# Layer 0 of a four-layer graph network: own rows and x are added by accumulating DMAs, nine instead of eight masks stand among the sums, and the steps between the matmuls are set anew

## The chip, the cores and the metric

The kernel runs on one core of one Trainium2 chip. A core has five engines that work side by side, each with its own queue of instructions: TensorE (PE, with its weight loads PEld), VectorE (DVE), ScalarE (ACT), GpSimd (POOL) and SyncE (SP, which here only issues DMAs). Each works its queue off in order; an instruction that waits holds up all that is queued behind it. The metric is the device time of one execution in microseconds (us), the median of several runs. Less is better.

## The reference, cut to what matters

There are N = 2708 nodes with 512 features each (x) and one adjacency matrix of 2708 x 2708 integers (adj). Four layers follow each other, each of the form x = layernorm(x + layer(x, adj)). The change concerns the first:

```python
Ab = A > 0
keep = Ab & (jnp.cumsum(Ab.astype(jnp.int32), axis=1) <= neibor_num)   # the first 64 neighbours of a row
cnt = keep.sum(axis=1, keepdims=True).astype(X.dtype)
nb_mean = (keep.astype(X.dtype) @ X) / jnp.maximum(cnt, 1.0)
xj = jax.nn.leaky_relu(nb_mean @ W_nb.T + b_nb)
xi = jax.nn.leaky_relu(X @ W_line.T + b_line)                          # "own rows"
layer = xi + jnp.where(cnt > 0, xj, 0)
...
x = _layernorm(x + layer, axis=-1)
```

Layer 1 takes the mean over all neighbours (the whole mask, not the first 64), with two weight matrices multiplied by halves of a third, W_comb. Layers 2 and 3 are attention layers, which the change leaves alone.

## The kernel before, in words

The rows are cut into 22 tiles of 128 (the last has 20 rows, `few`). D is 512, KD = 4 is its number of row blocks of 128. y = x @ W_nb.T is made first, so that layer 0's sum is keep @ y. y is held in two parts of a shortened float type, yH and yL, whose sum has the full precision: each matmul of the sums is done twice, once with each (`halves`). A mask tile is 128 rows of adj. It is loaded (`load_mask`, a DMA that POOL issues, 677 KB), counted (`count`, ACT, a sigmoid whose sum goes to cnts), placed (`place`, DVE, a running count that changes all entries behind the 64th neighbour, one scan and one multiplication for each part) and turned, since matmuls need it transposed: on PE (`turn_here`, 22 transposes and signs on ACT) or by a DMA that SP issues (`turn`, followed by `signs` on ACT). The result is maskT, in one byte for each entry.

**Stage A** (loop over the 22 tiles, L423 to L457): for each tile x is turned by PE (xT), multiplied by W_nb.T (kept by `keep_y`: yH by ACT at L272, yL by DVE at L277) and by W_line.T (own rows: DVE adds b_line at L452, POOL issues the store to r0_dram at L453). Beside it HERE = 14 masks are loaded, counted, placed in two halves and turned. The product's results lie in PSUM banks: own rows of an even tile and y of an odd tile, as well as the three banks of `turn_here`, come from four banks `acc` in rotation; the others have a bank each (pm0, pm1). u, the buffer of own rows, exists twice.

**Stage B** (L622 to L651): the sums. The tiles stand in blocks (`cuts`) of 4, 4, 4, 4, 4 and 2. In a block, step j (0 to 21) takes kT, a slice of the mask made by ACT (L471, a relu with the sign changed, so that only the first 64 neighbours remain), and adds its products with yH(j) and yL(j) to the banks of the block's tiles: eight matmuls (L639). At the end of a block ACT copies the banks to u0 to u3, divided by the count (`copy_of`, L620): two at once, two at the next block's first new kT. Between the steps the loop calls generators, one step of each at a time:

- `todo` is `finish` of the block before: fetch own rows (SP), add b_nb (L530), leaky (L229), leaky of own rows, add x to own rows by an accumulating DMA (POOL, L534), then `has` times u plus own rows (L536), the layer norm (`layer_norm`, with a power on POOL at L126), the store of x1 (L538), and the store of x1 as 16-bit words (`store_words`, L149 and L150), which a transposing DMA reads back in stage C.
- `both` is a chain of `other_masks` (the remaining eight masks: load, count in two halves, place in four, turn), `weights1` (the two weights of layer 1: rows of W_nb and W_self turned by PE at L139 and multiplied by halves of W_comb) and `vectors` (small vectors for layers 2 and 3).

PE's own order in stage A is written out by hand (`pe`, each of its instructions behind the one before); elsewhere a scheduler sets each engine's order by priority, and `tc.issue_after(x)` puts what stands in it behind x in the order.

**Stage C** (L652 to L672): layer 1's products, two for each tile (L300), from x1's words (`from_words`; the turned words are joined by ACT at L161). Behind it stage D makes layer 1's sums.

Of the kernel before, what the change touches and what calls it, by code (L numbers as in the profile page):

```python
# [20 lines left out]
P = 128  # L21
# [11 lines left out]
def kernel(  # L33
# [203 lines left out]
    with ExitStack() as phase:  # L237
# [68 lines left out]
        HERE = NT - 8  # L306
        cuts = [(b, min(b + 4, NT)) for b in range(0, NT, 4)]
        turns = range(NT)

        def load_mask(i, m):  # L310
            n = rows(turns[i])
            nc.gpsimd.dma_start(m[:n, :N], adj[turns[i] * P:turns[i] * P + n, :], max_dma_last_dim=N * 2)
            return m
# [43 lines left out]
        with ExitStack() as ph:  # L357
# [64 lines left out]
            due, stored = [], {}  # L422
            for t in range(NT):  # L423
# [18 lines left out]
                if now:  # L442
                    with tc.issue_after(stored[t - 1].ins) if t > 2 else nullcontext():
                        m = masks(counted)
# [3 lines left out]
                    with tc.issue_after(lows[t].ins):  # L448
                        place(counted, m, places, 0, 2)
                pm = product(xT, n, wlT, 1, pe, None if t % 2 else sums())  # L450
                u = sm.tile([P, D], F32, name="u")
                low = nc.vector.tensor_add(u[:n], pm[:n], b_line[:n])  # L452
                stored[t] = nc.gpsimd.dma_start(r0_dram[t * P:t * P + n, :], u[:n])  # L453
# [9 lines left out]
        with ExitStack() as ph:  # L463
# [10 lines left out]
            def other_masks():  # L474

                def room(i):
                    r = (ahead.tile([P, 2 * KD * (D + 2 * H)], BF16, name="w", tag="w", bufs=1) if i % 2 else
# [6 lines left out]
                got, left = {HERE: room(HERE)}, iter(())  # L484
                into = weight2.rearrange("p k c -> p (k c)").bitcast(BF16)[:, :NT * P].rearrange("p (t n) -> p t n", n=P)
                for _ in range(5):
                    yield
                for i in range(HERE, NT):
                    if i + 1 < NT:
                        got[i + 1] = room(i + 1)  # L490
# [8 lines left out]
                    for part in range(4):  # L499
                        place(i, m, places, part, 4)  # L500
# [6 lines left out]
                    for _ in left:  # L507
                        pass
                    turn(i, m, into)
                    left = chain(signs(i, into), map(twins, turns[i:i + 1], [turns[i] + 1]))  # L510
                    yield
                    if i < LAST:
                        yield
# [1150 lines left out]
```

## Time and profile before

| | us |
|---|---|
| median of 3 runs | 2873.31 (2872.43 to 2873.46) |
| the profiled execution | 2874.96 |
| its span, first to last instruction | 2873.2 |
| mean granted clock of PE | 0.996 |
| stage A | 0 to 188.8 |
| stage B | 188.8 to 455 |
| stage C | 455 to 614 |
| DVE busy, 0:50, 50:100, 100:150 | 30.65, 42.64, 43.13 |
| PE busy, 0:50, 50:100, 100:150 | 46.55, 46.45, 49.30 |

The profile is of one execution. Times in its views are microseconds from the span's start, unless marked ns. A line of the timeline holds start, duration, engine, line of the code, operation, output<-input and number; in brackets the engine's idle time ahead of it and what ended that. Durations of matmuls overlap, since they are pipelined: the time from start to start is what counts. A line of the windows holds the window, its length, busy time and number for PE, PEld, DVE, ACT and POOL, PE's granted clock (1.00 is full speed), the busy share of the DMA engines, and GB/s. A line of the waits holds engine, tile and line that waited, what it waited for, and the total, the number of times and the longest.

### The profile page before, as it was taken

The numbers are of one execution on the slowest core, as the hardware profiler recorded it, in microseconds if no ns is written. First come the engines' busy times: TensorE is split into PE (matmuls) and PEld (weight loads), VectorE is DVE, ScalarE is ACT, GpSimd is POOL, SyncE is SP. The second block draws the span as 40 slices with busy tenths as digits, with TensorE's granted clock in tenths as the row PEclk, the third lists the DMA queues.
The fourth block names the chain that finished last, engine by engine and source line by source line (L and its number), as shares of the span: only waits on it lengthen the run. The fifth ranks groups of instructions, "written<-read, shape, count | busy, mean of one in ns | idle before, by whom it ended". The sixth has DMA issues, their size and how long they took to land. (4 is left out here: it accounts for less than half of the span.)

```text
span 2873.2 us, 35718 instructions
## 1 busy us (share of the span) xinstructions
PE 2801.1 (97%) x13910; PEld 1556.9 (54%) x13910; DVE 1992.8 (69%) x2372; ACT 1525.4 (53%) x1754; POOL 294.1 (10%) x457
## 2 busy tenths in 40 slices
PE   9999999999999999999999999999999999999998
PEld 5458764458886434444466433444385555555565
DVE  6856755643336999999978999999954435445342
ACT  4646642232336999999956999999950000000011
POOL 1112421111110000000021000000300010100001
PEclk9999999999999999999999999999999999999999
DMA  7745657533323011111152110111161000000000
GB/s 181 151 105 124 148 145 172 123 96 122 107 82 69 27 38 38 42 48 42 36 175 84 41 41 36 56 36 35 35 173 52 4 26 15 26 15 16 15 19 25
DMA packets 203654, 202.64 MB, mean 71 GB/s; under 512 B 126823, under 2 KB 151724, under 8 KB 203476
## 3 DMA queue, kind: packets, MB, share of 16 engines
q1 hardware_dynamic: 167592, 122.05, 16.2%
q0 software_dynamic: 24880, 74.01, 9.5%
q10 hardware_dynamic: 11004, 4.22, 0.6%
q8 instruction: 111, 1.82, 0.3%
q14 instruction: 67, 0.55, 0.1%
HBM read 137.90 MB, written 55.66 MB: 67 GB/s over the span
## 5 line engine op out<-in xcount | busy, mean ns | idle before, releaser
L894 DVE SCALAR_TENSOR_TENSOR e<-v_bc,ucol,maskT 128x1408 f32<-128x1408 f32 (+3 forms) x798 | 1133.0, 1483 | 315.5 <-PE pn L1295 307.3
L923 ACT ACTIVATE c<-e,bcol 128x1300 fp8e4<-128x1300 f32 (+2 forms) x688 | 956.7, 1412 | 61.7 <-DVE e L894 16.8
L1095 PE MATMUL po<-e,R 128*64 128x512 f32 (+3 forms) x4224 | 893.9, 549 | 25.8 <-DVE e L894 23.6
L1095 PEld LDWEIGHTS po<-e,R 128*64 128x64 f32 (+1 forms) x4224 | 333.7, 136 | 553.0 <-issue 390.0
L1295 PE MATMUL pn<-e,R 128*128 128x512 f32 (+1 forms) x1008 | 396.4, 557 | 0.8
L1295 PEld LDWEIGHTS pn<-e,R 128*128 128x128 f32 x1008 | 177.8, 190 | 195.5 <-issue 181.2
L1224 ACT ACTIVATE w<-pl,b 128x256 f32<-128x256 f32 (+1 forms) x88 | 40.9, 465 | 365.7 <-PE pl L1222 365.7
L126 POOL TENSOR_TENSOR ln_rs<-ln_rs,half 128x1 f32<-128x1 f32 (+1 forms) x88 | 56.7, 644 | 1321.6 <-DVE ln_rs L125 1300.4
L815 PE MATMUL pm<-w,xT 128*128 128x264 f32 (+1 forms) x704 | 164.1, 388 | 3.4 <-ACT xT L141 1.3
L686 PE MATMUL acc<-yH,mf 128*128 128x512 f32 x418 | 162.9, 390 | 0.0
L686 PE MATMUL acc<-yL,mf 128*128 128x512 f32 x418 | 162.8, 390 | 0.0
L1222 PE MATMUL pl<-lin 128*128 128x256 f32 (+1 forms) x704 | 152.9, 372 | 0.6 <-DVE lin L1124 0.6
L1247 PE MATMUL pl<-lin,w 128*128 128x512 f32 x336 | 150.8, 593 | 0.0
L1222 PEld LDWEIGHTS pl<-lin 128*128 128x128 f32 x704 | 129.5, 190 | 31.0 <-issue 15.8
L815 PEld LDWEIGHTS pm<-w,xT 128*128 128x128 f32 (+1 forms) x704 | 129.9, 190 | 28.9 <-ACT xT L141 3.5
L683 ACT CAST mf<-maskT 128x1024 fp32r<-128x1024 fp8e4 (+1 forms) x66 | 64.5, 978 | 142.9 <-PE acc L686 140.1
L995 PE MATMUL pd<-c,parts_c 128*12 128x384 fp8e4 (+2 forms) x2688 | 128.4, 307 | 0.0
L471 ACT ACTIVATE kT<-maskT 128x512 fp32r<-128x512 fp8e4 x121 | 75.9, 629 | 97.5 <-PE acc L639 80.3
L639 PE MATMUL acc<-yH,kT 128*128 128x512 f32 x304 | 123.0, 404 | 3.8 <-ACT kT L471 2.9
L300 PE MATMUL acc<-w,xT 128*128 128x512 f32 (+1 forms) x256 | 117.3, 602 | 5.1 <-ACT xT L161 2.7
L639 PE MATMUL acc<-yL,kT 128*128 128x512 f32 x304 | 119.9, 394 | 0.0
L1313 ACT COPY lin<-pn 128x512 f32<-128x512 f32 (+1 forms) x12 | 5.8, 538 | 204.6 <-PE pn L1295 204.6
(291 smaller groups left out, 3007.9 us busy)
## 6 DMA issues: line engine op xcount, KB each, us to landing
v_bc<-v_dram SPq DMA_DIRECT2D x16, 704.0 KB
x_dram<-u POOLq DMA_DIRECT2D x42, 256.0 KB, 2.4
v_bc<-v_dram SPq DMA_DIRECT2D x16, 650.0 KB
m<-in_adj_dram POOLq DMA_DIRECT2D x14, 677.0 KB, 7.1
rows<-in_x_dram SPq DMA_DIRECT2D x21, 256.0 KB
r_dram<-u POOLq DMA_DIRECT2D x21, 256.0 KB, 3.5
rows<-r_dram SPq DMA_DIRECT2D x21, 256.0 KB
rows<-in_x_dram POOLq DMA_DIRECT2D x21, 256.0 KB, 4.8
```

The costliest lines, as they stand in the source:

```text
L300: order(nc.tensor.matmul(pm[:m], xT[:, k, :m], w[:, k, :], start=(k == 0), stop=(k == KD - 1)))
L471: made = nc.scalar.activation(kT, maskT[:, j:j + g, b[0] * P:b[0] * P + w], AF.Relu, scale=-1.0)
L639: nc.tensor.matmul(pa[t], kT[:, (t - b[0]) * P:(t - b[0] + 1) * P], y(j), start=(j == 0 and y is yH), stop=(j == LAST))
L686: nc.tensor.matmul(pa, mf[:, j - g0, :], y(j), start=(j == 0 and y is yH), stop=(j == LAST))
L815: nc.tensor.matmul(pm[a][:m, :D // 2 + heads], xT[:, k, :m], w[:, k, a, :D // 2 + heads], start=(k == 0), stop=(k == KD - 1))
L894: self.made = nc.vector.scalar_tensor_tensor(e[:, :w], v[:, :w], ucol[:, j, h:h + 1], maskT[:, j, c0:c0 + w], op0=OP.max, op1=OP.mult)
L923: nc.scalar.activation(c[:, :w], e[:, :w], AF.Sigmoid, bias=bcol[:, j, h:h + 1], scale=STEP, saturate=False)
L995: pe(nc.tensor.matmul(p[32 * g:32 * g + 12, :c1 - c0], parts_c[:, j, h, :], c[:, c0:c1], start=(i == 0 and h == hs[0]), stop=(i == NT - 1 ...
L1095: pe(nc.tensor.matmul(po[i][HO * k:HO * k + HO, :c1 - c0], R2[at, j, h * HO:(h + 1) * HO], e[at, a:a + c1 - c0], start=(i_ == 0), stop=(i_ ...
L1222: nc.tensor.matmul(pl[:, :w], self.lin1[:, k, f * P:(f + 1) * P], h[:, k, :w], start=(k == 0), stop=(k == KD - 1))
L1247: nc.tensor.matmul(pl[:n], gT[:, f, (t - t0) * P:(t - t0) * P + n], self.lin2[:, f, :], start=(f == 0), stop=(f == KF - 1))
L1295: nc.tensor.matmul(pn[k][:, :w], R2[at, j, k * P:(k + 1) * P], e[at, :w], start=(j == 0), stop=(j == NT - 1))
```

## The change

It touches layer 0 and the start of layer 1's weights:

- Stage A counts, places and turns 13 masks instead of 14, stage B nine instead of eight. PE turns seven in stage A instead of eight, DMAs six as before. The masks now come at tiles 1 to 3, 5 to 7, 9 and 10, 12 to 14, 16 and 17 (before: 1 to 4, 6 to 8, 10 to 13, 15 to 17).
- The leaky step on own rows is done in stage A, ahead of their store. The store of a tile is issued while the next tile is worked on, behind the next mask's load on POOL's queue.
- `finish` adds b_nb (times `has`), does the leaky step and then adds x and, two steps later, own rows to u in DRAM-to-buffer DMAs that accumulate. Nothing of own rows is fetched; the fetch on SP, L530, L536 and the leaky step on own rows are gone. The layer norm of a tile comes five steps, the store of its words six steps after its first. A step comes at odd j: 11 in a block.
- Of a block's end copies, two are made at once, one at j = 1 and one at j = 2, each behind the step's matmuls.
- The next mask is loaded behind the first of the four places of this one instead of ahead of this one's count. `twins` (a small copy of the mask's last rows) are sent later, in pairs.
- `weights1` begins at the first place of the last mask, and fetches its row blocks of weights one ahead; in SP's order three of them stand ahead of the last two masks' turns. The roles of two buffers (`w` and `spare`) are exchanged.
- `vectors` begins in stage C.

The diff, without what only renames a buffer's turn:

```diff
-        HERE = NT - 8
+        HERE = NT - 9
...
+            def store_own():
+                for t, u in own:
+                    stored[t] = nc.gpsimd.dma_start(r0_dram[t * P:t * P + rows(t), :], u)
+                own.clear()
+
             for t in range(NT):
...
                 if now:
-                    with tc.issue_after(stored[t - 1].ins) if t > 2 else nullcontext():
+                    with tc.issue_after(stored[t - 2].ins) if t > 2 else nullcontext():
                         m = masks(counted)
...
+                with tc.issue_after(loads[-1].ins):
+                    store_own()
                 pm = product(xT, n, wlT, 1, pe, None if t % 2 else sums())
                 u = sm.tile([P, D], F32, name="u")
-                low = nc.vector.tensor_add(u[:n], pm[:n], b_line[:n])
-                stored[t] = nc.gpsimd.dma_start(r0_dram[t * P:t * P + n, :], u[:n])
+                nc.vector.tensor_add(u[:n], pm[:n], b_line[:n])
+                low = leaky(u[:n], u[:n])
+                own.append((t, u[:n]))
+                if t >= LAST - 1:
+                    store_own()
...
             def other_masks():
...
-                for _ in range(5):
+                for _ in range(3):
                     yield
                 for i in range(HERE, NT):
-                    if i + 1 < NT:
-                        got[i + 1] = room(i + 1)
...
                     for part in range(4):
-                        place(i, m, places, part, 4)
+                        placed[:] = [place(i, m, places, part, 4)]
+                        if part == 0 and i == LAST:
+                            next(made_weights)
+                        elif part == 0:
+                            got[i + 1] = room(i + 1)
+                        if part == 0:
+                            for k in pairs:
+                                twins(k, k + 1)
+                            pairs.clear()
...
+                    if i > HERE:
+                        pairs.append(i - 1)
                     turn(i, m, into)
-                    left = chain(signs(i, into), map(twins, turns[i:i + 1], [turns[i] + 1]))
+                    left = signs(i, into)
                     yield
-                    if i < LAST:
-                        yield
+                    if HERE + 1 < i < LAST:
                         yield
...
             def finish(ts_, us):
-                r0s = early(1, len(ts_), lambda i: fetched(r0_dram, ts_[i], rows(ts_[i])))
-                for i, t in enumerate(ts_):
-                    n, u, r0 = rows(t), us[t], r0s(i)
-                    nc.vector.tensor_add(u[:n], u[:n], b_nb[:n])
-                    leaky(u[:n], u[:n])
-                    with tc.issue_after(low.ins):
-                        leaky(r0, r0)
-                    nc.gpsimd.dma_start(r0, x[t * P:t * P + n, :], accum_op=OP.add)
+                adds = []
+
+                def added(i, src):
+                    t = ts_[i]
+                    adds.append(nc.gpsimd.dma_start(us[t][:rows(t)], src[t * P:t * P + rows(t), :], accum_op=OP.add))
+
+                for i in range(len(ts_) + 6):
+                    with tc.issue_after(placed[0].ins) if placed else nullcontext():
+                        if i < len(ts_):
+                            t, n, u = ts_[i], rows(ts_[i]), us[ts_[i]]
+                            nc.vector.scalar_tensor_tensor(u[:n], b_nb[:n], has[:n, t:t + 1], u[:n],
+                                                           op0=OP.mult, op1=OP.add)
+                            leaky(u[:n], u[:n])
+                            added(i, x)
+                        if 0 <= i - 2 < len(ts_):
+                            added(i - 2, r0_dram)
+                        with tc.issue_after(adds[-1].ins):
+                            if 0 <= i - 5 < len(ts_):
+                                t = ts_[i - 5]
+                                n, u = rows(t), us[t]
+                                layer_norm(sm, u[:n], n, u[:n])
+                                nc.gpsimd.dma_start(x1_dram[t * P:t * P + n, :], u[:n])
+                            if 0 <= i - 6 < len(ts_) and ts_[i - 6] < LAST:
+                                t = ts_[i - 6]
+                                even = t % 2 == 0 and t < cuts[-1][0]
+                                store_words(words if even else ahead.tile([P, D], F32, name="rows", bufs=3),
+                                            x1_words, t, us[t])
                     yield
-                    nc.vector.scalar_tensor_tensor(u[:n], u[:n], has[:n, t:t + 1], r0, op0=OP.mult, op1=OP.add)
-                    layer_norm(sm, u[:n], n, u[:n])
-                    nc.gpsimd.dma_start(x1_dram[t * P:t * P + n, :], u[:n])
-                    yield
-                    store_words(r0 if t % 2 or ts_ == range(*cuts[-1]) else words, x1_words, t, u)
-                    yield
...
             def weights1():
...
-                order = [(w, m) for w in (l1_w_nb, l1_w_self) for m in range(KD)]
+                w_rows = early(1, 2 * KD, lambda i: fetched((l1_w_nb, l1_w_self)[i // KD], i % KD, P))
                 load_weight(first, l1_w_comb[D:2 * D, :], nc.sync)
-                nxt_rows = fetched(*order.pop(0), P)
+                w_rows(0)
...
-                        xT = transposed(ahead, ps_tr, nxt_rows, P, "xT")
-                        nxt_rows = fetched(*order.pop(0), P) if order else None
+                        xT = transposed(ahead, ps_tr, w_rows(i * KD + m), P, "xT")
...
+                        elif i and m == 0:
+                            twins(LAST - 1, NT)
...
-            todo, both = iter(()), chain(other_masks(), weights1(), vectors())
+            made_weights = weights1()
+            todo, both = iter(()), chain(other_masks(), made_weights)
...
-                        with tc.issue_after(nxt_made.ins):
-                            while copies:
-                                copy_of(*copies.pop(0))
                     kT = kTs.pop(0)
...
-                    if j % 3:
+                    if copies and j:
+                        with tc.issue_after(nxt_made.ins):
+                            copy_of(*copies.pop(0))
+                    if j % 2:
                         next(todo, None)
...
+            both = vectors()
+            placed.clear()
```

More of the change, by code (lines that the diff above doesn't have):

```diff
@@ L301, in product @@
             return pm
-        HERE = NT - 8
+        HERE = NT - 9
         cuts = [(b, min(b + 4, NT)) for b in range(0, NT, 4)]
         turns = range(NT)
+        loads = []
         def load_mask(i, m):
             n = rows(turns[i])
-            nc.gpsimd.dma_start(m[:n, :N], adj[turns[i] * P:turns[i] * P + n, :], max_dma_last_dim=N * 2)
+            loads.append(nc.gpsimd.dma_start(m[:n, :N], adj[turns[i] * P:turns[i] * P + n, :], max_dma_last_dim=N * 2))
             return m
@@ L421 @@
             counted = turned = 0
-            due, stored = [], {}
+            due, stored, own = [], {}, []
+            def store_own():
+                for t, u in own:
+                    stored[t] = nc.gpsimd.dma_start(r0_dram[t * P:t * P + rows(t), :], u)
+                own.clear()
             for t in range(NT):
@@ L476, in room @@
                 def room(i):
-                    r = (ahead.tile([P, 2 * KD * (D + 2 * H)], BF16, name="w", tag="w", bufs=1) if i % 2 else
+                    r = (ahead.tile([P, 2 * KD * (D + 2 * H)], BF16, name="w", tag="w", bufs=1) if (i - HERE) % 2 else
                          st.tile([P, 2 * KD * D], BF16, name="spare", tag="spare"))
@@ L482, in room @@
                     return m, r[:, NT * P:NT * P + N // 4 + 1]
-                got, left = {HERE: room(HERE)}, iter(())
+                got, left, pairs = {HERE: room(HERE)}, iter(()), []
                 into = weight2.rearrange("p k c -> p (k c)").bitcast(BF16)[:, :NT * P].rearrange("p (t n) -> p t n", n=P)
-                for _ in range(5):
+                for _ in range(3):
                     yield
                 for i in range(HERE, NT):
-                    if i + 1 < NT:
-                        got[i + 1] = room(i + 1)
                     m, places = got.pop(i)
@@ L545 @@
-            made1, signs_left = [], []
+                adds = []
[23 more added lines that the diff above has]
+                                            x1_words, t, us[t])
+                    yield
@@ L546 @@
+            made1, signs_left, placed = [], [], []
             acc, words = (sm.tile([P, D], F32, name="u") for _ in range(2))
@@ L549, in weights1 @@
             def weights1():
-                first, second = st.tile([P, KD, D], F32, name="spare", tag="spare"), weight2
+                first, second = weight(), weight2
                 bcs = []
-                order = [(w, m) for w in (l1_w_nb, l1_w_self) for m in range(KD)]
+                w_rows = early(1, 2 * KD, lambda i: fetched((l1_w_nb, l1_w_self)[i // KD], i % KD, P))
                 load_weight(first, l1_w_comb[D:2 * D, :], nc.sync)
-                nxt_rows = fetched(*order.pop(0), P)
+                w_rows(0)
                 nc.sync.dma_start(bias1, bcast(l1_b_comb, D))
@@ L561, in weights1 @@
                 for i, (bc, wc) in enumerate(zip(bcs, (first, second))):
-                    dst = weight() if i == 0 else st.tile([P, KD, D], F32, name="spare", tag="spare")
+                    dst = weight() if i else st.tile([P, KD, D], F32, name="spare", tag="spare")
                     made1.append(dst)
```

## The prediction

> **What bounds the kernel now.** I read the page from the top. Its first part gives the engines, its second the slices.
>
> ```profile
> span 2873.2 us, 35718 instructions
> PE 2801.1 (97%) x13910; PEld 1556.9 (54%) x13910; DVE 1992.8 (69%) x2372; ACT 1525.4 (53%) x1754; POOL 294.1 (10%) x457
> ```
>
> TensorE (PE) is busy 97% of the span, so only 72 us of PE's idle time and the time at a lower clock can be won without taking work from PE. The chain of work that ended last is of no help here: every share in it is 0%. I went to the windows instead, PE's busy time and granted clock (the PEclk column, behind POOL's) in stretches of 50 us. The change touches what runs from 0 to about 610 us. The stages are A (products, masks) to 189 us, B (layer 0's sums) to 455, C (layer 1's products) to 614.
>
> ```profile
> 50.00:100.00 50.00, 46.45 (x160) 22.83 (x159) 42.64 (x35) 28.66 (x39) 8.24 (x17) 0.97 0.80 155
> 200.00:250.00 50.00, 49.54 (x218) 40.43 (x217) 31.15 (x50) 30.18 (x48) 9.68 (x15) 1.00 0.39 85
> 300.00:350.00 50.00, 46.29 (x195) 37.01 (x194) 33.90 (x60) 29.17 (x46) 19.04 (x23) 0.97 0.71 150
> 350.00:400.00 50.00, 45.66 (x182) 34.06 (x181) 37.47 (x65) 23.99 (x42) 13.26 (x19) 0.97 0.58 150
> 450.00:500.00 50.00, 45.72 (x113) 21.66 (x112) 30.54 (x49) 11.68 (x15) 7.22 (x11) 0.97 0.77 164
> ```
>
> Four windows lose 3.5 to 4.3 us of PE and show the clock at 0.97, the others next to nothing. The waits of PE in the first 700 us, by releaser (total, times, longest), name them:
>
> ```profile
> PE ps_tr L139 <- DMA rows<-in_L_gnn_W_nb_dram: 4.3, 1, 4.3
> PE acc L336 <- DVE u L452: 3.6, 1, 3.6
> PE acc L639 <- ACT kT L471: 2.9, 1, 2.9
> PE acc L300 <- ACT xT L161: 2.7, 1, 2.7
> PE acc L300 <- DVE ln_rs L125: 1.6, 1, 1.6
> ```
>
> Each happens once. A stall costs more than its idle time. PE's timeline shows a sum's matmuls issued every 0.23 us; behind the 2.93 us of idle before 319.22 they come every 0.43 us, eight in a row:
>
> ```profile
> 319.22 0.50 PE L639 MATMUL acc<-yH,kT 128*128 128x512 f32 x1 [2.93 <-ACT kT L471]
> ...
> 320.25 0.63 PE L639 MATMUL acc<-yH,kT 128*128 128x512 f32 x1
> 320.68 0.63 PE L639 MATMUL acc<-yL,kT 128*128 128x512 f32 x1
> ```
>
> So that stall costs 2.93 + 8 x 0.20 = 4.5 us. Behind 3.55 us of idle at 90.45 and behind 2.70 us at 487.15 a product takes 5.40 us for 3.60 to 3.70 (1.7 and 1.8 more); behind 1.58 us at 477.35 it takes 3.67. I count the after-effect only for idle times above 2 us. The Trainium skill, "TensorE: Matmul & The Clock Gate", section "What's actually happening", states that the clock halves after an idle window of about 3.4 us and that the window runs freely. Idle times of 2.70 and 2.93 us have halved it here. Were shorter ones than 3.4 us free of it, the gain below would be 3.4 us smaller; I go by the rows.
>
> **What can go, by stage.** Stage A: 3.55 + 1.7 at 90.45, 0.69 at 120.50 (L340): 5.9. Stage B: 0.46 (236.18), 0.27 (271.94), 0.79 (313.08, ACT's copy L620), 4.5 (319.22), 4.34 + 1.6 for the weight rows at 385.03, 0.69 at 439.73: 12.6. Stage C: 1.58 (477.35), 2.70 + 1.8 (487.15), 0.17 and 0.63 (510.09, 514.38): 6.9. Together 25.4 us. One mask fewer is turned by PE (L336, 22 transposes): rows of 1.42 to 1.49 us, 1.45. **The ceiling of the gain is 26.9 us**; all else that the change moves lies beside PE and counts only where it makes PE wait.
>
> **Stage A.** DVE loses one mask's placing (two scans, two multiplies: 2.98 + 3.03 + 2 x 0.86 = 7.7) and gets 22 leaky steps (L229, 0.68 each, 0.60 from start to start: 13). It was busy 42.6 of 50 us in the two worst windows, so this isn't free. The stall at 90.45 came so: DVE stood 2.87 us before 69.59 for a count (L317), whose mask load stood on POOL's queue behind the store of own rows (the largest POOL wait of this stage is for u of L452, 116 us in 20 times). Then it worked without a gap through two and a half masks to 90.40, when u of the tile (L452) came free, and the third bank of the transposes needed it at 86.89. After the change the load stands before that store, so I take the 2.87 off; the run of masks 12 to 14 has the same form. From the first scan to u of its third tile: 8.4 (first mask with y's subtraction) + 9.55 (second: 7.7 with u's addition, y's subtraction and the new leaky at 0.6 each) + 3.7 (scan, addition) = 21.65 us, where before it was 20.8. So u comes 20.8 - 21.65 + 2.87 = 2.0 us earlier than before, and 3.55 becomes **1.5 us**, below what halves the clock. In the run of tiles 5 to 7 the turn comes at tile 7 behind one and a half masks, 12.1 us: I take 0.7. At the even tiles (4, 10, 18, 20) the third bank is that of two tiles ago, no wait. Kept: 2.2 of 5.9. Bounds: 0 (both waits vanish) to 2 x (3.55 + 1.7) = 10.5 (the count comes no earlier, both stalls are full ones). The store of own rows a tile later waits for nothing that PE needs: u has two buffers, the next use is two tiles (14 us) on, and a store lands 3.5 us after issue.
>
> **Stage B, block starts.** Before, copies 2 and 3 of a block's end (L620) and a count's half could stand together ahead of kT: on ACT one copy waited 1.86 us for an old x_dram store and then a 1.41 us count went before kT:
>
> ```profile
> 316.56 0.69 ACT L620 ACTIVATE u<-pm,rkeep 128x512 f32<-128x512 f32 x1 [1.86 <-DMA x_dram<-u]
> 317.14 1.41 ACT L317 ACTIVATE w<-w,gate 128x1354 bf16<-128x1354 bf16 x1
> 318.46 0.19 ACT L317 ACTIVATION_READ_ACCUMULATOR w<-w,gate 128x1 f32 x1
> 318.55 1.14 ACT L471 ACTIVATE kT<-maskT 128x512 fp32r<-128x512 fp8e4 x2
> ```
>
> After it, step j of a block (eight matmuls, 1.815 us) gets one thing each: copies 0 and 1 and kT(1) at the end (0.6 each: 1.84 us against 1.815), copy 2 with half a count and kT(3) (5.1 against 5.4), copy 3 with the other half (0.64 + 1.6 + 0.6 more: 7.75 against 7.26). That is 0.5 us of wait at four blocks, **2.0 us**, and no store is waited for, since a finish ends at step 19 of 22. Bounds: 0 and 4 x 0.8 + 4.5 (one such stall remains) = 7.7.
>
> **Stage B, finishing.** Per tile DVE loses the addition of b_nb (0.67), a leaky (0.68) and L536's wait for the landing (18.4 us of DVE's idle in 20 times); the addition with has takes L536's place (0.74). SP loses 21 fetches of own rows. POOL gets 22 accumulating DMAs. An issue of this kind takes 0.91 us (321.36), the landing a median of 4.8. Two sums to one tile must follow each other, so POOL's order holds x(0), x(1), the load of the next mask, own rows (0) (waits for x(0)'s landing), (1), x(2), own rows (2), x(3), own rows (3) (waits 4.8 us), and behind these the power of the layer norm (L126) and the stores. PE needs none of them until stage C, except through masks and weights. The mask load, 6.3 to 8.0 us, is issued 14.5 us or more (eight steps) ahead of its count: **6.5 us to spare**. The ninth mask's work (DVE 8.5, ACT 3.2 + 3.1) lies beside PE, DVE being busy 31 to 37 of 50 us here and relieved of 28. Cost 0; with the cover gone see the first rival.
>
> **Stage B, weights.** The rows of W_nb, issued at 382.10 behind the fetches of own rows and awaited at 385.03, now stand (three of four) on SP ahead of the last two masks' turns, and own rows are no longer there: 5.9 and 0.7 go. One place is tight, the fourth row block, which needs the buffer of tile 13's words. These are made at step 15 of the block (15 x 1.815 + two weight products of 3.43 = 34 us), their store lands 3.9 us on, the fetch takes 2.9: 41 us. PE asks at step 17 (17 x 1.815 + 3 x 3.43 + transposes 1.4 = 43). I keep 0.5 us; bounds 0 and 5.9.
>
> **Stage C.** vectors() starts here, so its first loads no longer stand on SP before the transposes of x1_words: ACT stood 13.0 us for one at 485.94. And DVE no longer holds for the accumulating DMA (2.69 us before 473.35) that led to the 1.58. Seven loads now come between two of the transposes, about 28 us before PE needs the later one. I keep 1.0 of 6.9; bounds 0 and 6.9.
>
> **Sum.** Kept: 2.2 + 2.0 + 0.5 + 1.0 = 5.7. Gain 26.9 - 5.7 = 21.2 us. The profiled execution took 2874.96 (span 2873.2, 1.8 around it), so it would be 2853.8; the median of the runs shown is 2873.31, 1.65 lower, and by it **2852.1**, which I give as 2852.0. All lower bounds: 2846.4. All upper bounds (10.5 + 7.7 + 5.9 + 6.9 = 31 kept): 2877.4.
>
> **Rivals.** *One: POOL is late with the mask loads, and the change is slower.* Two more accumulating DMAs a tile, with waits for their landings in the queue, hold POOL; the load of the next mask comes more than 6.5 us late; the count stands at ACT's head and kT behind it. Place: steps 1 and 2 of a block. Price: the row at 319.22, 4.5 us, for each of eight loads, 36 us: 2852 + 36 = 2888. It decides from about five such stalls on. For it: POOL's wait for L126 is 119 us in 22 times, and landings went up to 9.1 us. Against: in POOL's order nothing that waits for a landing stands directly ahead of the load at a block's start, POOL is busy 10%, and its issues take 0.91 us beside a busy DVE. 15%. The Trainium skill speaks against the change here: "SBUF — State Buffer", section "SBUF: two separate sides", says that GpSimd can't write the descriptors of a DMA that it issues while VectorE runs certain operations, and that a DMA issued on SP is immune. By that page, estimated at one scan (1.6 us) for each of 22 DMAs that leave SP, POOL would lose 35 us in all, 6 a block, which is about the time to spare; no row here shows such a block.
>
> *Two: the stalls go halfway.* Stage A's fuller DVE stalls PE in full at tiles 7 and 15 (10.5 for 2.2 us, 8.3 more), or one stall of 4.5 us stays at a block start as well: 2860 to 2865, say 2863. For it: DVE 85% busy in stage A with 5 us net to do on top. Against: its idle time of 13.1 us for counts, which the earlier loads shorten. 17%.
>
> *Three: the stalls only move.* Four long ones made 20 of the 25 us, each by one late buffer; a new order can have four others: 2870. 11%.
>
> **How the numbers follow.** Forecast, 13 to 27 us gained: 57%. Rival two: 17%. Three: 11%. One: 15%. About 0.2% (5.7 us) is what a measurement of this kernel can tell from no change. Faster: 0.57 + 0.17 = 0.74; same 0.11; slower 0.15. The range leaves out the slower case and a little beyond the ceiling: 2845 to 2874, which takes in the third rival and the upper bounds but for the last 3 us.
>
> **What would show it.** Right: the windows 300 to 400 and 450 to 500 at 49 us or more of PE and clock 1.00; no wait of PE for W_nb rows or for xT L161; at most two waits of 1 to 2 us for u in stage A; DVE without the waits for own rows and x. Wrong: PE waits for kT with ACT waiting for a mask load (rival one); a wait above 2 us at the turns of tiles 7 or 15 (two); a new wait of 3 us or more for weights or xT (three).

## The result and the profile after

The changed kernel is slower: 2881.8 us (median of 22 runs, 2876.1 to 2886.92) against 2874.31 (22 runs, 2870.09 to 2878.24); the ratio is 1.0024, 95% interval 1.0018 to 1.0031. Forecast were 2852.0 and a range from 2845 to 2874, so the result lies outside it. The profiled execution took 2884.09 us, 2.3 above the median. The head of its page:

```profile
span 2882.3 us, 35604 instructions
...
PE 2802.1 (97%) x13888; PEld 1557.6 (54%) x13888; DVE 1984.2 (69%) x2355; ACT 1525.6 (53%) x1756; POOL 306.2 (11%) x479
```

DVE and PE have fewer instructions, as the diff says, and PE is as busy as before in spite of 22 fewer transposes: a product at half the clock counts as busy for longer (5.40 us instead of 3.60 to 3.70). The windows (busy time of PE, PEld, DVE, ACT and POOL, then granted clock, DMA share and GB/s):

```profile
50.00:100.00 50.00, 50.00 (x172) 24.59 (x171) 47.45 (x43) 31.94 (x42) 8.27 (x17) 1.00 0.79 166
100.00:150.00 50.00, 46.92 (x161) 23.13 (x160) 42.42 (x39) 26.62 (x35) 7.41 (x15) 0.97 0.83 170
250.00:300.00 50.00, 45.75 (x194) 37.09 (x193) 29.54 (x46) 29.55 (x47) 20.21 (x31) 0.97 0.85 160
350.00:400.00 50.00, 43.02 (x163) 32.41 (x162) 33.11 (x61) 23.20 (x40) 18.33 (x26) 0.90 0.78 147
450.00:500.00 50.00, 45.61 (x121) 23.37 (x120) 27.04 (x45) 13.34 (x17) 8.52 (x13) 0.97 0.83 176
```

The loss at 50 to 100 has moved to 100 to 150, the sums lose in 250 to 300 what they didn't before, and 350 to 400 is worse, with the clock at 0.90. PE's waits in the first 700 us:

```profile
PE acc L672 <- ACT kT L484: 9.6, 3, 4.4
PE pm L672 <- ACT kT L484: 7.3, 3, 3.6
PE acc L338 <- DVE u L462: 3.1, 1, 3.1
...
PE acc L300 <- DVE u L705: 1.2, 1, 1.2
```

The waits for the rows of W_nb, for xT and for ln_rs are gone, as forecast. In their place PE waits six times for kT, 16.9 us, four of them for 3.4 to 4.4 us with half clock behind each (1.7 to 2.2 us more). One place shows PE's wait and what ACT did ahead of it, at the start of the third block:

```profile
281.26 0.50 PE L672 MATMUL acc<-yH,kT 128*128 128x512 f32 x1 [4.25 <-ACT kT L484]
```

```profile
274.12 0.62 ACT L484 ACTIVATE kT<-maskT 128x512 fp32r<-128x512 fp8e4 x1
278.60 0.69 ACT L656 ACTIVATE u<-acc,rkeep 128x512 f32<-128x512 f32 x1 [3.85 <-DMA x_dram<-u]
279.18 1.41 ACT L319 ACTIVATE spare<-spare,gate 128x1354 bf16<-128x1354 bf16 x1
280.50 0.19 ACT L319 ACTIVATION_READ_ACCUMULATOR spare<-spare,gate 128x1 f32 x1
280.59 1.14 ACT L484 ACTIVATE kT<-maskT 128x512 fp32r<-128x512 fp8e4 x2
```

It is the picture of 316 us in the kernel before: a copy waits for the store of x1 out of its buffer, then a count goes ahead of kT. The finish of the block before isn't done. POOL and DVE, in that block, show why:

```profile
241.93 0.85 POOL L552 DMA_DIRECT2D u<-in_x_dram  x1 [1.06 <-DVE u L229]
249.51 0.85 POOL L552 DMA_DIRECT2D u<-r_dram  x1 [6.73 <-DMA u<-in_x_dram]
250.04 1.19 POOL L552 DMA_DIRECT2D u<-in_x_dram  x1
256.91 0.86 POOL L552 DMA_DIRECT2D u<-r_dram  x1 [5.67 <-DMA u<-in_x_dram]
257.47 1.51 POOL L126 TENSOR_TENSOR ln_rs<-ln_rs,half 128x1 f32<-128x1 f32 x2
...
273.37 0.58 POOL L569 DMA_DIRECT2D x_dram<-u  x1 [0.88 <-DVE u L128]
```

```profile
248.92 0.15 DVE L125 TENSOR_SCALAR ln_rs<-ln_mv 128x1 f32<-128x1 f32 x1
258.41 1.15 DVE L128 TENSOR_SCALAR u<-u,ln_mv,ln_rs 128x512 f32<-128x512 f32 x2 [9.34 <-POOL ln_rs L126]
```

The own-row add of the third tile waits 6.7 us at POOL's head for that tile's x to land; the fourth tile's x is queued behind it, its own rows wait 5.7 us more, and behind these stand the powers of the first two tiles, ready since 249. DVE waits 9.3 us at its own head for them, and the next mask's places, the layer norms of the last two tiles and their stores (the last issued at 273.4) come behind that. That store lands at 278.5, and the copy at 278.60 waited for it: the finish ends some 9 us after the next block has begun (its first copies stand at 269.3).

It is so all through stage B. The longest waits of POOL and DVE for landings and powers there (186 to 470 us), of the changed kernel first, then of the kernel before:

```profile
POOL u L552 <- DMA u<-in_x_dram: 62.0, 14, 8.4
```

```profile
DVE u L128 <- POOL ln_rs L126: 35.3, 13, 12.4
DVE ln_st L121 <- DMA u<-r_dram: 20.5, 7, 6.6
```

```profile
DVE u L128 <- POOL ln_rs L126: 9.2, 17, 1.1
```

The stages in the profiled executions (us). Stage A ends with PE's first matmul of the sums, C with its first of layer 1's sums; the end of B is taken 0.7 us behind the last matmul of layer 0's sums, in every row alike:

| | stage A ends | B lasts | C lasts | behind C |
|---|---|---|---|---|
| before | 188.8 | 267.1 | 157.6 | 2259.7 |
| after | 186.5 | 278.7 | 151.9 | 2265.2 |

B lost 11.6, A and C won 2.3 and 5.7. Behind C, where no instruction differs, 5.5 us were lost, and 3.1 of them go with the kernel, not with the execution: from DVE's last instruction, behind which only the last store is left, to the end of the span it is 11.0 to 11.2 us in all four kernels that add x and own rows of every tile by accumulating DMAs (the changed one, e1, e5, e9 below), 9.9 in e13, which does so for half of the tiles, 8.6 and 8.8 in e10 and e7, which store own rows so, and 7.7 to 8.0 in the other eleven. No run shows why. The other 2.4 us arise around 2100 us; e14, whose late layers are those of the kernel before, loses as much there, so I count them as a difference between executions.

### The profile page after: what moved, and what is told of

Read it like the earlier page. It is cut to its first block, busy times and chain, and to the rows that moved or that the text cites. A ratio compares the mean times of both kernels' runs of the same rounds, so it can differ in the third digit from the quotient of the medians.

```text
span 2882.3 us, 35604 instructions
## 1 busy us (share of the span) xinstructions
PE 2802.1 (97%) x13888; PEld 1557.6 (54%) x13888; DVE 1984.2 (69%) x2355; ACT 1525.6 (53%) x1756; POOL 306.2 (11%) x479
```

## The experiments

**Theory A**: two accumulating DMAs in series for each tile hold POOL's queue and DVE, and a finish outlasts its block. **Rival B**: the counts, which now stand at block starts ahead of kT, are the cause whatever the finish does. **Rival C**: the DMA traffic is too dense. Each group of runs had the kernel before beside it, whose median lay between 2874.3 and 2876.0 us; so differences of under 2 us between rows say nothing. Stages are those of the one profiled execution. Medians, ratios to the kernel before (95% intervals) and stages (us):

| run | median us | ratio | A ends | B | C |
|---|---|---|---|---|---|
| e1 layer norm freed | 2876.84 | 1.0002 (0.9993-1.0011) | 185.0 | 271.4 | 153.5 |
| e2 no own rows | 2858.76 | 0.9938 (0.9925-0.9952) | 187.0 | 257.7 | 153.7 |
| e3 own rows fetched | 2862.52 | 0.9953 (0.9939-0.9966) | 187.9 | 265.1 | 150.3 |
| e4 before, vectors later | 2873.86 | 0.9998 (0.9989-1.0007) | 190.0 | 266.2 | 157.0 |
| e5 POOL reordered | 2875.28 | 0.9999 (0.9989-1.0009) | 186.0 | 264.1 | 150.3 |
| e6 = e3, xT copies later | 2864.21 | 0.9961 (0.9947-0.9975) | 186.7 | 254.7 | 159.5 |
| e7 one add, early copy of x | 2874.13 | 0.9995 (0.9986-1.0004) | 199.3 | 255.3 | 153.2 |
| e8 before, stage A's part | 2863.76 | 0.9952 (0.9939-0.9966) | 188.9 | 256.8 | 154.8 |
| e9 copies 2, 3 later | 2901.02 | 1.0089 (1.0073-1.0104) | 186.5 | 294.7 | 154.3 |
| e10 one add, x copied by tile | 2866.67 | 0.9968 (0.9955-0.9980) | 193.9 | 259.9 | 151.4 |
| e11 before, leaky step only | 2867.05 | 0.9966 (0.9953-0.9979) | 188.7 | 257.0 | 154.6 |
| e12 = e3, eight masks | 2878.88 | 1.0011 (1.0003-1.0020) | 189.4 | 266.3 | 163.3 |
| e13 last two tiles fetched | 2870.01 | 0.9986 (0.9978-0.9995) | 185.0 | 267.9 | 151.4 |
| e14 = e8, turn moved | 2863.27 | 0.9958 (0.9945-0.9971) | 188.7 | 256.2 | 155.8 |
| e15 = e3, turn moved | 2859.81 | 0.9948 (0.9935-0.9961) | 183.9 | 263.2 | 150.3 |
| e16 = e15, xT and vectors | 2852.72 | 0.9918 (0.9905-0.9932) | 183.3 | 258.9 | 150.3 |

### The second accumulating DMA: e1, e2, e3, e5, e13

e1 frees the layer norm from the last own-row add:

```diff
-                        with tc.issue_after(adds[-1].ins):
+                        with nullcontext():
```

> The changed kernel, but the layer norm is no longer ordered behind the last own-row add: on POOL the powers of a block's first two tiles now stand ahead of the own-row add of its fourth tile. Theory A (two accumulating DMAs in series for each tile hold POOL, and with it the powers, DVE and the end of a block's finish): DVE's wait for the power, 9.3 us at 258 us, falls to about 4, the store that ACT's copy waits for comes some 5 us earlier, and the time falls by 6 to 12 us from the changed kernel's 2882, to 2870 to 2876. Rival B (the counts that now stand at the start of each block ahead of kT on ACT are the cause, whatever the finish does): within 2 us of 2882. Rival C (the DMA traffic is too dense and landings are long): within 3 us.

5.0 us faster than the changed kernel, just short of what A expected of it, outside what B and C did. DVE's longest wait for a power fell to 4.1 us, as A had it, and PE's waits for kT at the first three block starts to 0.5 us or less; but at 371 us PE waits 7.5 us for kT behind the signs of a late turn (3.6 at 379 in the changed kernel), so the gain is what is left of two changes. e2 leaves the own-row adds out:

```diff
-                        if 0 <= i - 2 < len(ts_):
-                            added(i - 2, r0_dram)
```

> The changed kernel without the own-row adds of layer 0 (own rows are left out of the output; one accumulating DMA a tile is left, x). Theory A: POOL's waits for a landing (66 us in 16 times) go, the copies at block starts wait for no store, stage B loses 15 to 20 us of its 278, time 2862 to 2867. Rival B: 2879 to 2882, the waits for kT stay. Rival C: lower too, by the share of the traffic, about 5 us.

23 us faster. The counts stand where they stood; PE's waits for kT in e2:

```profile
PE acc L670 <- ACT kT L484: 2.9, 3, 1.6
...
PE pm L670 <- ACT kT L484: 0.3, 1, 0.3
```

3.2 us for 16.9: **B falls** (own rows are missing in e2's output). e3 fetches own rows on SP and adds them on DVE ahead of the layer norm (0.67 us a tile):

```diff
+                r0s = early(0, len(ts_), lambda i: fetched(r0_dram, ts_[i], rows(ts_[i])))
...
-                        if 0 <= i - 2 < len(ts_):
-                            added(i - 2, r0_dram)
+                        if 0 <= i - 4 < len(ts_):
+                            r0s(i - 4)
...
+                                nc.vector.tensor_add(u[:n], u[:n], r0s(i - 5))
                                 layer_norm(sm, u[:n], n, u[:n])
```

> The changed kernel, but own rows are fetched by a plain DMA of SP's queue one step ahead and added by DVE ahead of the layer norm (0.67 us a tile); x is still added by the accumulating DMA. The same bytes move as in the changed kernel. Theory A: like the run without own rows but for 22 x 0.67 us of DVE beside PE: 2862 to 2870. Rival B: 2879 to 2884. Rival C: as the changed kernel, 2879 to 2884, since the traffic is the same.

19.3 us faster with the same bytes: **C falls**, as far as the number of bytes goes. In the profiled executions 13.6 of it lie in B, 1.6 in C and 5.4 behind C, while A is 1.4 longer. What differs is in the issues (last number: median us to landing), first of the changed kernel, then of e3:

```profile
u<-in_x_dram POOLq DMA_DIRECT2D x21, 256.0 KB, 6.2
u<-r_dram POOLq DMA_DIRECT2D x21, 256.0 KB, 5.2
```

```profile
rows<-r_dram SPq DMA_DIRECT2D x21, 256.0 KB
u<-in_x_dram POOLq DMA_DIRECT2D x21, 256.0 KB, 4.6
```

One accumulating DMA a tile lands in 4.6 us, and nothing is queued behind its landing; two take 6.2 and 5.2 in series. POOL's waits for x to land, 62.0 us in 14 times within 186 to 470 us, are not there in e3. Is it the place on POOL's queue or the two landings? e5 keeps both adds and puts them in a better order:

```diff
-                adds = []
+                adds, xs_ = [], []
...
                             added(i, x)
+                            xs_.append(adds[-1])
                         if 0 <= i - 2 < len(ts_):
-                            added(i - 2, r0_dram)
-                        with tc.issue_after(adds[-1].ins):
+                            with tc.issue_after(xs_[-1].ins) if i >= len(ts_) else nullcontext():
+                                added(i - 2, r0_dram)
+                        with nullcontext():
```

> The changed kernel with both accumulating DMAs kept, but on POOL the own-row adds of a block's third and fourth tile stand behind the x add of the fourth, and the powers of the first two tiles ahead of the last own-row add. Theory A in the form that the order on POOL's queue is the price: POOL's waits for a landing inside stage B fall from 53 us (the run with the freed layer norm) to about 35, stage B from 271 to 267 us, time 2870 to 2874. Theory A in the form that two landings one after the other are the price, wherever they stand: as the run with the freed layer norm, 2875 to 2879.

2875.28: by the time, the form with the two landings (2875 to 2879). But its profiled execution was the fastest of 11 (2867.1, up to 2883.48), and there POOL's waits for a landing are down to 20.4 us, further than the form with the order had forecast, PE's waits for kT are about those of e3 (0.3, 0.3, 0.3, 1.4 and 5.2 us for 0.2, 0.3, 0.3, 1.2 and 6.9), and B is as short as e3's. That execution loses only behind C (2264.8 us for 2259.8 in e3). Where the slower ten lose more is in no trace. So the price of the second add as a whole is shown, 19 us; a better order on POOL wins 5.0 (e1) to 6.5 us (e5) of it; that the rest is the second landing is argued, not shown. Nor does a run fetch own rows by a plain DMA on POOL's queue, which would tell the queue from the accumulation. e13 fetches own rows for a block's last two tiles only:

```diff
+                r0s = early(0, len(ts_), lambda i: fetched(r0_dram, ts_[i], rows(ts_[i])) if i > 1 else None)
...
-                        if 0 <= i - 2 < len(ts_):
+                        if 0 <= i - 2 < min(2, len(ts_)):
                             added(i - 2, r0_dram)
+                        if 0 <= i - 4 < len(ts_):
+                            r0s(i - 4)
...
+                                if i - 5 > 1:
+                                    nc.vector.tensor_add(u[:n], u[:n], r0s(i - 5))
```

> The changed kernel, where own rows of a block's first two tiles are still added by accumulating DMAs, and those of its other two are fetched by SP and added by DVE. If the late end of a finish (the third and fourth tile's chain of two landings, with the powers of the first two tiles queued behind it) is the price, this is as good as fetching all: 2860 to 2866. If every second accumulating DMA costs its share, wherever it stands in the block, half of the way: 2870 to 2874.

2870.0, the edge of "halfway": 11.8 us for the last two tiles' adds and 7.5 for the first two's. The loss isn't the late end of the finish alone. In the profiled executions (5.3 us apart) e13 still loses 4.2 to e3 behind C, 2.8 in B and 1.1 in C, while its A is 2.9 shorter.

### How the late finish reaches PE: e9, e6, e12

e9 makes the waiting third and fourth copies later, since their banks are free for long:

```diff
-                    if copies and j:
+                    if copies and j in (4, 6):
```

> The changed kernel, but the third and fourth copy of a block's end are made behind steps 4 and 6 of the next block instead of 1 and 2; their banks aren't needed earlier. If the late finish reaches PE through ACT's copies, which wait for the last store out of their buffer and stand ahead of kT, the waits for kT at 281, 323 and 367 us (8.7 us and 3.2 of half clock) go: 2868 to 2872. The waits at 379 (signs behind a late turn) and 456 us (layer 1's words) stay. If the finish reaches PE in other ways (DVE late with the masks), 2876 or more.

A clear miss: 19 us slower. At most one copy waits 1.2 us for a store now, but the x adds of these tiles start later too, and with them all that follows. PE waits 12.5 us at 388 for kT behind signs (a late turn; ACT waited 13.2 us for that DMA) and 9.8 at 475, where ACT waits for layer 1's words. Between 309 and 361 it also waits 5.8 us in four times for the first two copies of a block's end, which are late here, and 2.6 for kT at 318, where a mask load is late (ACT waits 3.4 us for it). So the copies are one path only; the finish itself must end earlier.

In the last block ACT's first copies of layer 1's words (L161) stand ahead of kT and wait for the transposing DMAs: 4.4 us of PE's time in the changed kernel (455.80), 6.9 in e3. e6 puts them behind the last kT of e3:

```diff
-                xT = xTs(t)
+                with tc.issue_after(nxt_made.ins):
+                    xT = xTs(t)
```

> The run with fetched own rows, and ACT's first copies of layer 1's turned words put behind the last kT of the sums. If those copies, which stand ahead of kT and wait for transposing DMAs, cost PE the 6.9 us that it still waits for kT in the last block (and 1.7 of half clock), time is 2853 to 2858. If the loss only moves into stage C, whose first product then waits for the copy, 2860 to 2864.

B falls from 265.1 to 254.7 and C grows from 150.3 to 159.5: nothing is won. DVE in stage C tells where it went:

```profile
458.35 0.69 DVE L645 TENSOR_TENSOR weight<-weight 128x512 f32<-128x512 f32 x1 [1.83 <-DMA weight<-in_L_gnn_W_dram]
...
462.14 0.69 DVE L645 TENSOR_TENSOR weight<-weight 128x512 f32<-128x512 f32 x1 [1.78 <-DMA weight<-in_L_gnn_W_dram]
...
464.79 0.68 DVE L277 TENSOR_TENSOR yL<-acc,yH 128x512 fp32r<-128x512 f32 x1
```

The vectors' weights stand at DVE's head ahead of yL, and PE waits for yL (2.2, 1.5, 0.8 us). e12 has eight masks in e3:

```diff
-        HERE = NT - 9
+        HERE = NT - 8
```

> The run with fetched own rows, with 14 masks in stage A and eight among the sums. If the ninth mask costs nothing among the sums, as I had it, one more mask's transposes on PE (1.45 us) and its placing come back: 2862 to 2868. If the ninth mask's counts and signs on ACT are part of the loss, 2855 to 2860.

Neither: with a mask fewer the weights begin sooner (PE is ready for their first product at 360.5 us, in e3 at 376.1), but the fetch of W_comb does not (358.8 and 359.4), and PE waits 8.5 us for it, and later 10.2 for xT. It says nothing of the ninth mask's own cost, which stays open.

### One part alone: e4, e8, e11

e4 starts the vectors in stage C:

```diff
-            todo, both = iter(()), chain(other_masks(), weights1(), vectors())
+            todo, both = iter(()), chain(other_masks(), weights1())
...
+            both = vectors()
             xTs = from_words(x1_words, x1_dram, ps_tr)
```

> The kernel before with one part of the change: the small vectors of layers 2 and 3 start in stage C instead of the last block of sums. If this part alone gave stage C's gain (158.4 to 152.6 us), time is 2867 to 2870 and ACT's wait of 13.0 us for the transposed words goes. If the gain came from the finish without DVE's waits for accumulating DMAs, 2873 to 2876.

The second case: the interval takes in 1, stage C lasts 157.0, and ACT's wait of 13.0 us for the transposed words is still there, 12.8 us. This part alone did not give the gain in C. e8 is stage A's part in the kernel before, with 14 masks (`store_own`, `own` and the mask load behind `stored[t - 2]` as in the change):

```diff
+                with tc.issue_after(loads[-1].ins):
+                    store_own()
...
-                low = nc.vector.tensor_add(u[:n], pm[:n], b_line[:n])
-                stored[t] = nc.gpsimd.dma_start(r0_dram[t * P:t * P + n, :], u[:n])
+                nc.vector.tensor_add(u[:n], pm[:n], b_line[:n])
+                low = leaky(u[:n], u[:n])
+                own.append((t, u[:n]))
...
-                    with tc.issue_after(low.ins):
-                        leaky(r0, r0)
```

> The kernel before with stage A's part alone: the leaky step on own rows in stage A, their store a tile later behind the next mask's load; still 14 masks there. If the earlier mask loads are worth what I took (2.9 us of DVE's wait) and the leaky steps cost less, stage A ends at 185 to 188 us and time is 2870 to 2874. If DVE's fuller stage A is the price, stage A ends at 190 or later, 2876 to 2882.

12.3 us faster, more than either case, and stage A isn't shorter at all. e11 moves the leaky step only:

```diff
-                low = nc.vector.tensor_add(u[:n], pm[:n], b_line[:n])
+                nc.vector.tensor_add(u[:n], pm[:n], b_line[:n])
+                low = leaky(u[:n], u[:n])
...
-                    with tc.issue_after(low.ins):
-                        leaky(r0, r0)
```

> The kernel before with the leaky step on own rows moved to stage A, and nothing else (their store is where it was). If the gain of the run with stage A's part (2876 to 2864) comes from the finish, where DVE no longer waits for fetched own rows ahead of POOL's add, 2862 to 2867. If it comes from the later store and the earlier mask loads, 2872 to 2876, or above for the 13 us of added DVE work in stage A.

8.8 us faster (at the edge of the first case), B 257.0: the gain is in the sums. Its profiled execution, 2862.37, is 4.7 us below its median. Before, DVE waited at its head for fetched own rows (29.0 us in 8 times) and POOL's add of x behind that. Without the leaky step there, the stall at 319 us is down from 2.93 to 0.98 us and that at 385 (4.34) is gone. This step alone does most of what I had put down to the new block starts and the weights.

### One add a tile without a fetch: e7, e10

e7 adds x to own rows in DRAM:

```diff
+            for t in range(0, NT, 4):
+                with tc.issue_after(weights_made.ins):
+                    nc.sync.dma_start(r0_dram[t * P:min(t * P + 4 * P, N), :], x[t * P:min(t * P + 4 * P, N), :])
...
-                    stored[t] = nc.gpsimd.dma_start(r0_dram[t * P:t * P + rows(t), :], u)
+                    stored[t] = nc.gpsimd.dma_start(r0_dram[t * P:t * P + rows(t), :], u, accum_op=OP.add)
...
-                            added(i, x)
-                        if 0 <= i - 2 < len(ts_):
-                            added(i - 2, r0_dram)
+                            added(i, r0_dram)
```

> The changed kernel, but x is copied to own rows' place in DRAM at the start (SP, six DMAs), stage A's own rows are stored by accumulating DMAs, and the finish adds once for each tile. If one accumulating DMA a tile is harmless in the finish (as in the run without own rows) and in stage A, 2857 to 2863. If accumulating stores hold the two buffers of own rows in stage A or the early copy delays the first tiles, stage A is over 190 us and time 2866 or more.

B is 255.3, C 153.2, as good as e2, but PE waits 12.3 us at 43 us for rows of x behind the early copy. e10 copies a tile at a time, in the loop over tiles:

```diff
+                with tc.issue_after(fetches[-1].ins):
+                    nc.sync.dma_start(r0_dram[t * P:t * P + n, :], x[t * P:t * P + n, :])
```

> As the run with one add a tile, but x is copied to own rows' place tile by tile, on SP behind the fetches of each tile. If the 12.3 us that PE waited for rows of x at 43 us came from the early copy alone, stage A ends at 187 to 189 us and time is 2857 to 2862. If the extra traffic in stage A delays the masks, stage A is above 192 us and time above 2865.

Stage A ends at 193.9, with five stalls of 0.6 to 3.1 us instead of two: the finish's gain is paid back there in part.

### Stage A's stall, and the best version: e14, e15, e16

The transposes at tile 15 wait for u of tile 14, whose DVE work began at 116 us:

```profile
116.07 2.98 DVE L326 TENSOR_TENSOR_SCAN places<-m,over 128x1354 bf16<-128x1354 bf16 x1 [1.07 <-ACT m L319]
...
136.81 0.67 DVE L462 TENSOR_TENSOR u<-acc,bias 128x512 f32<-128x512 f32 x1
```

```profile
137.53 0.59 PE L338 MATMUL acc<-identb,m 128*128 128x128 bf16 x6 [3.08 <-DVE u L462]
138.05 5.40 PE L300 MATMUL pm<-weight,xT 128*128 128x512 f32 x8
```

e14 and e15 move that turn to the next tile, which is even (in e14: turn 5, tile 9):

```diff
-                while turned < min(HERE, counted - (t + 2 < NT and not by_dma(turned))):
+                while (turned, t) != (9, 15) and turned < min(HERE, counted - (t + 2 < NT and not by_dma(turned))):
```

> The run with stage A's part alone (2863.8), but the fifth PE-side turn that came at tile 9 comes at tile 10, where the third bank of the transposes is that of own rows two tiles ago. If my reading of the stall there is right (u of the tile before, late behind half a mask's placing on DVE), PE's wait for u of 3.1 us and the half clock behind it (1.7 us) go: 2858 to 2861. If DVE's lateness finds PE elsewhere (y's difference, or the mask of the next load comes late), 2862 to 2867.

> The run with fetched own rows (2862.5), but the turn that came at tile 15 comes at tile 16. By the same reading 2856 to 2860; if the lateness goes elsewhere, 2861 to 2865.

In e15 stage A ends 4.0 us earlier and the wait for u is gone (1.6 us for maskT at 164 come in its place). In e14 the stall for u goes as well, but the next mask's load comes late (ACT waits 6.5 us for it) and PE waits 2.2 us for maskT, with half clock behind it: nothing won. e16 takes e15, e6's line, and ties each step of vectors to its tile:

```diff
-                nc.vector.tensor_add(u[:n], pm[:n], bias1[:n])
-                next(both, None)
+                plus = nc.vector.tensor_add(u[:n], pm[:n], bias1[:n])
+                with tc.issue_after(plus.ins):
+                    next(both, None)
```

> The changed kernel with own rows fetched and added by DVE, the turn of tile 15 at tile 16, ACT's first copies of layer 1's words behind the last kT of the sums, and one step of the small vectors for each tile, behind the addition of that tile. The run with the first two of these took 2859.8 and still waited 6.0 us for kT in the last block (with half clock 7.6). If the copies' place and DVE's waits for the vectors' weights made that loss, 2851 to 2855. If stage C gives it back again, as in the run with the copies alone, 2858 to 2862.

2852.7 us, 0.8% below the kernel before, with C at 150.3: the loss in the last block was one of its own and need not move. PE's waits in its first 625 us:

```profile
PE pm L674 <- ACT kT L484: 3.0, 2, 2.7
PE acc L292 <- ACT u L290: 2.2, 2, 1.5
PE acc L300 <- ACT maskT L342: 1.5, 1, 1.5
...
PE acc L674 <- ACT kT L484: 0.6, 2, 0.3
```

## Why the prediction was wrong, step by step

- **The step that failed: "Stage B, finishing ... Cost 0", and with it "no store is waited for, since a finish ends at step 19 of 22".** I wrote that own rows (3) wait 4.8 us on POOL with the power of the layer norm behind them, and asked only whether the mask load would be late. I didn't follow DVE, which waits at its own head for that power, nor add up the landings: 7.6 + 7.4 us from the issue of the third tile's x to that of the fourth's own rows, a wait of DVE of 9.3 us meanwhile, and a last store that landed at 278.5, 9 us into the next block. Cost of the own-row adds: 19.3 us (against e3), 23 (against e2), of which 5.4 and 5.7 lie behind C in the profiled executions. Without own-row adds B lasted 257.7 us, where the forecast makes 267.1 - 12.6 + 2.5 = 257.0; with them 278.7. The sign that I had named, DVE without waits for own rows and x, did not come (20.5 us for own rows in B).
- **Rival one** had the right resource and the wrong place. Mask loads weren't late; POOL's waits for landings reached PE through the copies and a late turn, which shrink without them (e2, e3). The wait for layer 1's words isn't theirs, as far as is known: e3, without those waits, has more of it (6.9 us for 4.4). That its number, 2888, came near is luck: not one of its eight late loads occurred.
- **Block starts.** About right where the finish is in time: 0.2 to 0.3 us at the first three block starts in e3 and 1.2 at the fourth: 2.0 in all, as forecast, though not 0.5 each.
- **Stage A.** Forecast 5.15 us (3.7 and the transposes' 1.45), measured 2.3. The term that failed is "so I take the 2.87 off": the run of scans began 18.4 us ahead of the need (116.07 to 134.44), where before it was 17.3. ACT, not the load, sets the count: it worked signs for 2.8 us ahead of it (110.68). The place was right (tile 15; at tile 7 no wait), the DVE chain too (21.4 us to u, 21.65 forecast); the stall was 3.08 for 1.5, the half clock followed it (1.7 us; in e1 and e13, with the same stall, it did not, and A ended at 185.0), and 0.83 us came at the turn of tile 4, where I had none.
- **Weights.** The waits for W_nb and W_self rows went, as forecast; so they do in e11, where only the leaky step moves (0.8 left).
- **Stage C.** 5.7 us for 5.9 forecast, but not for the reason given, so the number is luck: vectors alone left C at 157.0 and ACT's wait for the words as it was (e4), while the leaky step alone brought C to 154.6 (e11). Which part made the rest isn't shown. And the words' copies took 4.4 us and half clock from the last block, a wait that I hadn't listed.
- **Sum.** Forecast 21.2 us less, measured 7.5 more: 28.7 apart. In the profiled executions B is 21.7 above its forecast, A 2.9, and 5.5 lie behind the changed part, where I had put nothing.
- **Readings.** Two were off without weight in the sum: DVE's 18.4 us at L536 in stage B came in 5 waits, not 20, and the window from 0 to 50 loses 3.45 us as well, at full clock.

## What to carry to other kernels

A step taken off a busy engine and given to a DMA is not free when something must wait for its landing: lay the landings of one buffer end to end, follow who stands behind each wait on the issuing queue, and then who waits for that. Two accumulating DMAs to one buffer left 62 us of waits for landings on POOL's queue here; a fetch ahead on another queue and one addition (0.67 us of DVE) left none of these, and 6.3 us of DVE's waits for the fetched rows (e3). And test the parts of a compound change singly: here one moved instruction gave most of a gain that another part took back twice over.

## What the runs showed of the hardware

An accumulating DMA of 256 KB landed in a median of 4.5 to 4.8 us when each tile had one (before, e2, e3, e7, e10), and in 5.7 to 6.4 for x with 5.2 to 6.5 for own rows when each had two (the changed kernel, e1, e5). The kernels with two in series also varied more from run to run (the changed one 2876.1 to 2886.9 in 22 runs, e1 2871.7 to 2882.2 and e5 2867.1 to 2883.5 in 11) than those with one (before 2870.1 to 2878.2 in 22, e7 2871.8 to 2878.7 in 11); I have no run that says why.

The half clock does not go by the length of a stall alone. The same idle time of 3.08 us of PE at tile 15 had it behind it in the changed kernel and not in e1:

```profile
137.66 0.59 PE L338 MATMUL acc<-identb,m 128*128 128x128 bf16 x6 [3.08 <-DVE u L462]
138.19 3.70 PE L300 MATMUL pm<-weight,xT 128*128 128x512 f32 x8
```

The product took 5.40 us there and 3.70 here, and 3.70 in e13. In e10 an idle time of 1.80 us (73.33) was followed by 5.40 us already; 2.08 us in e9 (528.66) and 2.22 in e6 (456.66) were not (3.70 and 3.67). So the 2 us from which the prediction counted the after-effect is no threshold: between 1.8 and 3.1 us these runs show both, and the 1.7 us make part of the difference between two executions.
